# The last 65 keys of a cross-attention, split into 64 in half-array products and one by itself

## The chip, the cores and the metric

The kernel runs on one core of one Trainium2 chip. The metric is the device time of one execution in microseconds. The unchanged kernel took 3020.45, 3022.51 and 3024.7 us in three runs, a median of 3022.51.

A core has these engines, under the names that the profile uses: PE (TensorE, matrix products) with PEld (its weight loads), DVE (VectorE), ACT (ScalarE), POOL (GpSimd) and SP (SyncE, which issues most DMAs). A name with a q behind it (SPq, ACTq) is that engine's queue as an issuer of DMAs. They run side by side and wait for each other through semaphores.

## The reference

The program is a two-layer Perceiver block. Only its first piece changes, a cross-attention of 8 batches, each with 64 queries of width 512 over 1601 keys, in 16 heads of width 64:

```python
q = x @ Wq.T                              # (8, 64, 1024)
k, v = split(context @ Wkv.T, 2)          # (8, 1601, 1024) each
sim = einsum('bhid,bhjd->bhij', q, k) * 64**-0.5
sim = where(mask, sim, -max)
out = einsum('bhij,bhjd->bhid', softmax(sim), v)
return out @ Wout.T + b_out
```

All of it is in fp32. What follows it (a second attention with a Fourier transform and convolutions, experts, another cross-attention, another attention and a quantized feed-forward) is not touched.

## The kernel before

The keys are never projected. The query side is multiplied with the key weights once (`qk`, 512 x 512 for eight heads of a batch), so that the scores are `context @ qk`; and `softmax @ context` is made first (`a`) and multiplied with the value weights afterwards (`v_ps`).

The work goes in 16 **steps**, a step being one batch and one half of the heads, so that the 512 columns of a step are 8 heads by 64 queries. The loop over `step` at the end of `l0_xattn` lays out, for each step: load `qk` (`queries_of`, from a DRAM copy) and the columns of the context (`load_columns`), then `scores` of this step, then `attend` of the step before, then `softmax` of this step. So the matrix engine works at `attend` of the last step while the vector and scalar engines work at the softmax of this one. The Tile framework's scheduler turns this program order into one fixed list per engine, and interleaves the two steps at their seams. I call the seam at which `scores` of one step ends and `attend` of the step before begins a **passage**, and number it by the step whose `qk` is loaded there, 1 to 15.

1536 of the 1601 keys are multiplied by Strassen-Winograd's method in blocks of 256 x 512: seven products instead of eight, on quarters (`Quarters`, `Run`). GpSimd makes the sums of the context's quarters (`Quarters.left`, lines 136 to 139), and those of the queries' quarters (`right_of`, lines 222 to 225). Results of the products are taken out of PSUM by ScalarE (copies, line 439) and VectorE (sums, line 444), and VectorE keeps a running maximum `m` (line 460).

The other 65 keys, the **tail**, are multiplied plainly: in `scores` by four products of 128 columns of weights by 512 columns (line 472; 63 of the 128 weight columns are zeros), and in `attend` by eight products with 65 rows by 256 columns (line 605), four for each of two blocks, placed among the others by the class `Mixed`, which adds them to the same PSUM banks where it can.

PSUM is split into four pools of two banks each: `ps_x`, `ps_y`, `ps_z` for the seven products, and `ps_m` for all else: tail, `m_ps` (transposes of the maximum, line 498), `top_ps` (its broadcast, line 503), sums and values. The tile `qk` has one buffer: its next load is issued when the last product that reads it is done. Each fp32 product appears in the trace as two matmul records; an "x4" of a row is two products.

Of the kernel before, what the change touches and what calls it, by code (L numbers as in the profile page):

```python
# [120 lines left out]
NPAIR = LAST // 2  # L121

# [19 lines left out]
def l0_xattn(K, x, d, ternary, kept):  # L142
# [7 lines left out]
    with ExitStack() as es:  # L150
# [10 lines left out]
        ctxT_tail = wp.tile([P, DC, P], F32, tag="ctxT_tail", name="ctxT_tail")  # L161
        nc.gpsimd.memset(ctxT_tail, 0.0)
        ctx_tail = wp.tile([P, D], F32, tag="ctx_tail", name="ctx_tail")
        bias = wp.tile([P, B, NK], F32, tag="bias", name="bias")
        qk_all = [dp.tile([P, n, DC, NG, 2, S], F32, tag=f"qk_all{n}", name="qk_all") for n in (2, B - 2)]
        sp = es.enter_context(tc.tile_pool(name="a_s", bufs=2))
        tp = es.enter_context(tc.tile_pool(name="a_t", bufs=2))
        zp = es.enter_context(tc.tile_pool(name="a_z", bufs=1))

# [41 lines left out]
        def load_tails(b):  # L211
            nc.sync.dma_start(
                ctxT_tail[:, :, :TAIL], d["ctxT"][b, :, LAST * P :].rearrange("(c p) n -> p c n", p=P)
            )
            nc.sync.dma_start(ctx_tail[:TAIL], d["ctx"][b, LAST * P :, :])
# [78 lines left out]
        wqT = sp.tile([P, NK, HALF], F32, tag="s", name="wqT")[:, :8, :].rearrange("p (c j) n -> p c (j n)", j=2)  # L294
        wk = sp.tile([P, NK, HALF], F32, tag="s", name="wk")[:, :NG, :]
# [15 lines left out]
        m32 = wp.tile([B * NK, P], F32, tag="m32", name="m32")  # L311
        nc.scalar.dma_start(m8, d["mask"])
        load_tails(0)
        ctxT = load_columns(0)
        place = [tp.tile([P, 4, 3, QH], F32, tag="pt", name="stage").rearrange("p a b q -> p (a b q)") for _ in range(2)]
# [25 lines left out]
        for j in range(2):  # L341
# [17 lines left out]
        nc.vector.tensor_copy(m32, m8)  # L359
        ps = ps_m.tile([P, B * NK], F32, tag="mm", name="m_ps")  # L360
        nc.tensor.transpose(ps, m32, K.ident[: B * NK, : B * NK])
        nc.vector.tensor_scalar(
            bias.rearrange("p b k -> p (b k)"), ps, 1.0, -MASKED, ALU.subtract, ALU.mult
        )

# [65 lines left out]
        class Scores:  # L431
# [25 lines left out]
            def c21(self, ps):  # L457
                nc.scalar.activation(self.s[:, self.k + 1, :QH], ps, AF.Identity, bias=self.bias[1], scale=1.0)  # L458
                for k in (self.k, self.k + 1):
                    nc.vector.tensor_max(self.m, self.m if k else self.s[:, LAST, :], self.s[:, k, :])  # L460

        def scores(b, qkt, ctxT):
            qk, qt = qkt
            s = sp.tile([P, NK, HALF], F32, tag="s", name="s")
# [5 lines left out]
            ps = ps_m.tile([P, HALF], F32, tag="mm", name="s_ps")  # L470
            for c in range(DC):
                nc.tensor.matmul(ps, lhsT=ctxT_tail[:, c, :], rhs=qk[:, c, :], start=c == 0, stop=c == DC - 1)  # L472
            nc.scalar.activation(s[:, LAST, :], ps, AF.Identity, bias=bias[:, b, LAST : LAST + 1], scale=1.0)
            run = Run()
            for i in range(NPAIR):

                def mul(ps, n, start, i=i):
                    for e in range(2):
                        nc.tensor.matmul(  # L479
                            ps,  # L480
                            lhsT=ctxT[i][:, Quarters.LEFT[n], ts(e, P)],
                            rhs=right[n][:, e, :],
                            start=start and e == 0,
                            stop=e == 1,
                            skip_group_check=not start,
                        )

                run.add(mul, Scores(s, m, b, i))
                some(2)
                next(aside, None)  # L490
            run.end()
            return s, m
# [13 lines left out]
        def softmax(s, top):  # L506

            parts = []
            for k in (LAST, *range(0, LAST, 2)):
                n = min(2, NK - k)  # L510
# [15 lines left out]
            nc.vector.tensor_add(total[:TAIL], total[:TAIL], s[:TAIL, LAST, :])  # L526
            return parts, total

        class Mixed:
# [3 lines left out]
            def __init__(self, a, m, first, tail):  # L533
                self.a, self.m, self.first, self.tail = a, m, first, tail
# [4 lines left out]
            def keep(self, out, ps, h, n):  # L539
                if self.first:  # L540
                    nc.scalar.copy(out, ps)
                else:
                    nc.vector.tensor_add(out, ps, self.of(h, n))
# [7 lines left out]
            def p5(self, out, ps):  # L551
                if self.first:
                    w = ps_m.tile([P, HALF], F32, tag="mm", name="w_ps")[:, :QH]
                    self.tail(w, 1, 1, True)
                    nc.scalar.copy(out, w)
                    nc.vector.tensor_add(out, ps, out)
                else:
                    self.keep(out, ps, 1, 1)

            def c11(self, ps, p1):  # L560
                if self.first:
                    self.tail(ps, 0, 0, False)
                nc.vector.tensor_add(self.of(0, 0), ps, p1)

            def c12(self, ps, u2):
                if self.first:
                    self.tail(ps, 0, 1, False)
# [5 lines left out]
            def c21(self, ps):  # L573
                if self.first:
                    self.tail(ps, 1, 0, False)
                    nc.scalar.copy(self.of(1, 0), ps)
                else:
                    nc.vector.tensor_add(self.of(1, 0), ps, self.of(1, 0))

        def attend(half, s, soft, ctx, o, first):  # L580

            a = tp.tile([P, DC, HALF], F32, tag="a", name="a", bufs=1)
            wvT = wp.tile([P, DC, HALF], F32, tag="wvT", name="wvT")
# [3 lines left out]
            parts, total = soft  # L587
            run = Run()
            for part, right in enumerate(parts):
                pairs = range(3 * part, 3 * part + 3)  # L590
                for m in range(2):
# [12 lines left out]
                    def tail(ps, h, n, start, m=m):  # L604
                        nc.tensor.matmul(
                            ps,
                            lhsT=ctx_tail[:TAIL, ts(2 * h + m, P)],
                            rhs=s[:TAIL, LAST, ts(n, QH)],
                            start=start,
                            stop=True,  # L610
                            skip_group_check=not start,
                        )

                    run.add(mul, Mixed(a, m, part == 0, tail))
# [9 lines left out]
            nc.vector.reciprocal(rs, sums)  # L624
# [11 lines left out]
            nc.vector.tensor_mul(o[:, ts(half, NG // 2)], ps, rs)  # L636
# [22 lines left out]
        for step in range(2 * B + 1):  # L659
            if step < 2 * B:  # L660
                b, half = divmod(step, 2)
                if step:
                    now, ctxT = queries_of(b, half), load_columns(b, half)
                    if half == 0:
                        nc.sync.dma_start(
                            ctxT_tail[:, :, :TAIL], d["ctxT"][b, :, LAST * P :].rearrange("(c p) n -> p c n", p=P)
                        )
                s, m = scores(b, now, ctxT)
# [3 lines left out]
            if before:  # L672
                b0, half0 = divmod(step - 1, 2)
                attend(half0, *before, load_rows(b0), o[:, :, b0 % 2, :], step == 1)
                if half0 and b0 + 1 < B:
                    nc.sync.dma_start(ctx_tail[:TAIL], d["ctx"][b0 + 1, LAST * P :, :])
            if step < 2 * B:
                before = s, softmax(s, top)
# [1666 lines left out]
def layout(i):  # L2345
# [10 lines left out]
        "mask": np.pad(i["mask_BxS2_bf1"].view(np.uint8), ((0, 0), (0, NK * P - NKV))).reshape(B * NK, P),  # L2356
        "L0x_WqT": i["L0_xattn_Wq"].T,
# [72 lines left out]
```

## Time and profile before

| what | value |
|---|---|
| median of three runs | 3022.51 us |
| the profiled execution, its device time | 3019.59 us |
| its span, first to last instruction | 3017.8 us |
| PE busy | 2953.5 us (98% of the span), 15393 records |
| DVE, ACT, POOL busy | 61%, 28%, 28% of the span |
| granted TensorE clock, mean | 0.991 |

The cross-attention fills the first 1478 us of the span. The page's 40 slices show how even that stretch is:

```profile
PE   8999999999999999999999999999999999999897
PEld 6767778888888888888654446778788888888664
DVE  4845555666666666666533343487677676676838
ACT  2322232222232322222201222233333323323224
POOL 3341341424335342424110002322412404224011
```

A digit is the busy share of a slice of 75 us in tenths. The first twenty slices are the cross-attention: the matrix engine has no slice under 9 after the first, the vector engine stands mostly at 5 to 6, and the other two lower.

### The profile page before, as it was taken

The page shows a single profiled execution, that of the slowest core. Times are in us where ns is not written, and L with a number is a line of the kernel's source. Part 1 is how long each engine was busy: PE and PEld are TensorE (multiplying, and loading weights), DVE is VectorE, ACT ScalarE, POOL GpSimd, SP SyncE. Part 2 cuts the span into 40 slices and gives each one's busy share as a digit, 9 for nine tenths or more (in the row PEclk, how much of TensorE's full clock was granted, in tenths as well). Part 3 has the DMA queues.
Part 4 walks back from the last instruction along what each step waited for, and adds up shares of the span by engine and source line. Part 5 has one row for each costly group of instructions (what it writes and reads, how often), then busy time and mean ns, then how long its engine had stood idle before and what let it go on. Part 6 is the DMA issues. An engine that isn't in the chain of part 4 may idle for free.

```text
span 3017.8 us, 40186 instructions
## 1 busy us (share of the span) xinstructions
PE 2953.5 (98%) x15393; PEld 2263.7 (75%) x15393; DVE 1828.9 (61%) x3122; ACT 844.9 (28%) x1620; POOL 850.1 (28%) x766
## 2 busy tenths in 40 slices
PE   8999999999999999999999999999999999999897
PEld 6767778888888888888654446778788888888664
DVE  4845555666666666666533343487677676676838
ACT  2322232222232322222201222233333323323224
POOL 3341341424335342424110002322412404224011
PEclk9999999999999999999999999999999999999989
DMA  9275465544545564442649974202112021020260
GB/s 331 83 231 168 126 218 186 191 161 167 190 157 188 189 206 161 170 140 93 230 167 351 342 257 147 82 27 76 37 58 78 5 90 53 29 90 11 108 83 15
DMA packets 287725, 429.43 MB, mean 142 GB/s; under 512 B 50830, under 2 KB 187030, under 8 KB 283310
## 3 DMA queue, kind: packets, MB, share of 16 engines
q1 hardware_dynamic: 272345, 388.56, 38.6%
q10 hardware_dynamic: 14549, 36.21, 3.5%
q8 instruction: 122, 2.00, 0.3%
q0 software_dynamic: 640, 2.10, 0.2%
q14 instruction: 69, 0.57, 0.1%
HBM read 351.77 MB, written 75.04 MB: 141 GB/s over the span
## 4 chain that ended last, share of the span: by engine, by line
PE 92%; DVE 4%; DMA 1%; ACT 1%; issue 1%; POOL 0%; SPq 0%; POOLq 0%; DVEq 0%; ACTq 0%
PE x_ps L595 11%; PE x_ps L1529 11%; PE x_ps L479 11%; PE y_ps L1529 8%; PE s_ps L1699 6%; PE z_ps L479 5%; PE z_ps L595 5%; PE oe_ps L1244 4%; PE h_ps L1217 4%; PE acc L1754 3%; PE y_ps L595 3%; PE y_ps L479 3%; PE s_ps L472 2%; PE qk_ps L257 1%; PE v_ps L629 1%; PE sum_ps L1576 1%
## 5 line engine op out<-in xcount | busy, mean ns | idle before, releaser
L1589 POOL TENSOR_TENSOR r<-r,minus_half 128x52 f32<-128x52 f32 x32 | 277.0, 8673 | 552.6 <-DVE r L1588 552.6
L479 PE MATMUL x_ps<-qt,ctxT 128*128 128x256 f32 x1152 | 284.6, 381 | 2.3 <-DVE s L444 2.3
L595 PE MATMUL x_ps<-pt,ctx 128*128 128x256 f32 x1152 | 280.3, 381 | 0.0
L136 POOL TENSOR_TENSOR ctx<-ctx 128x256 f32<-128x256 f32 x96 | 74.2, 772 | 626.4 <-DMA ctx<-in_ctx 375.9
L479 PEld LDWEIGHTS x_ps<-qt,ctxT 128*128 128x128 f32 x1152 | 217.3, 190 | 40.2 <-issue 4.7
L595 PEld LDWEIGHTS x_ps<-pt,ctx 128*128 128x128 f32 x1152 | 216.5, 189 | 33.7 <-DVE a L568 1.6
L1699 PE MATMUL s_ps<-qb,kT 128*128 128x256 f32 x832 | 201.3, 382 | 0.1
L460 DVE TENSOR_TENSOR m<-m,s 128x512 f32<-128x512 f32 x176 | 138.4, 786 | 95.2 <-ACT s L458 92.8
L1699 PEld LDWEIGHTS s_ps<-qb,kT 128*128 128x128 f32 x832 | 155.0, 190 | 27.5 <-issue 4.9
L444 DVE SCALAR_TENSOR_TENSOR s<-y_ps,bias,p 128x256 f32<-128x256 f32 x96 | 46.4, 483 | 153.4 <-PE y_ps L479 153.0
L1709 DVE TENSOR_TENSOR s<-s_ps,r 128x512 f32<-128x512 f32 x192 | 126.7, 683 | 13.9 <-PE s_ps L1699 11.6
L511 DVE TENSOR_TENSOR s<-s,top_ps 128x1024 f32<-128x1024 f32 (+1 forms) x112 | 123.2, 1136 | 12.0 <-PE top_ps L503 12.0
L1739 DVE TENSOR_TENSOR s<-s,top_ps 128x1792 f32<-128x1792 f32 x64 | 117.9, 1884 | 16.5 <-PE top_ps L1735 16.3
L1740 ACT ACTIVATE s<-s 128x1792 f32<-128x1792 f32 x64 | 101.1, 1591 | 66.2 <-DVE s L1739 66.2
L1754 PE MATMUL acc<-s,v 128*64 128x128 f32 x1664 | 115.6, 280 | 3.7 <-ACT s L1740 3.7
L512 ACT ACTIVATE s<-s 128x1024 f32<-128x1024 f32 (+1 forms) x112 | 110.3, 996 | 29.7 <-DVE s L511 25.7
L1754 PEld LDWEIGHTS acc<-s,v 128*64 128x64 f32 x1664 | 98.1, 139 | 27.0 <-issue 22.6
L1217 PE MATMUL h_ps<-w,tok 128*128 128x512 f32 x256 | 117.3, 593 | 0.0
L1244 PE MATMUL oe_ps<-w,hT 128*128 128x512 f32 x256 | 115.6, 593 | 0.0
L525 DVE TENSOR_TENSOR total<-total,s 128x512 f32<-128x512 f32 x160 | 111.3, 695 | 3.7
L1236 ACT ACTIVATE hT<-hT_ps,L0f_be,L0f_g 128x128 f32<-128x128 f32 x128 | 55.4, 456 | 179.8 <-PE hT_ps L1235 116.9
L479 PE MATMUL x_ps<-qk,ctxT 128*128 128x256 f32 x384 | 103.5, 387 | 0.0
(470 smaller groups left out, 6116.1 us busy)
## 6 DMA issues: line engine op xcount, KB each, us to landing
w<-in_L0f_W SPq DMA_DIRECT2D x64, 1024.0 KB, 6.8
ctx<-in_ctx SPq DMA_DIRECT2D x192, 256.0 KB, 3.4
kept<-ctxT SPq DMA_DIRECT2D x48, 896.0 KB, 10.1
ctxT<-kept SPq DMA_DIRECT2D x48, 896.0 KB, 7.8
ctxT<-kept SPq DMA_DIRECT2D x24, 1792.0 KB, 7.8
ctxT<-in_ctxT SPq DMA_DIRECT2D x96, 256.0 KB, 4.9
wvT<-in_L0x_WvT SPq DMA_DIRECT2D x16, 1024.0 KB, 8.8
qk<-qk_all SPq DMA_DIRECT2D x15, 1024.0 KB, 6.6
```

The lines of the kernel that those rows point to most:

```text
L460: nc.vector.tensor_max(self.m, self.m if k else self.s[:, LAST, :], self.s[:, k, :])
L479: nc.tensor.matmul(ps, lhsT=ctxT[i][:, Quarters.LEFT[n], ts(e, P)], rhs=right[n][:, e, :], start=start and e == 0, stop=e == 1, skip_group ...
L511: nc.vector.tensor_sub(s[:, k : k + n], s[:, k : k + n], top.unsqueeze(1).to_broadcast([P, n, HALF]))
L595: nc.tensor.matmul(ps, lhsT=ctx[pair][:, Quarters.LEFT[n], ts(m, P)], rhs=right[n][:, i, :], start=start and i == 0, stop=i == 2, skip_gro ...
L1217: nc.tensor.matmul(ps, lhsT=self.tok[:, c, :], rhs=self.w1[n][:, c, :], start=c == 0, stop=c == DC - 1)
L1244: nc.tensor.matmul(ps, lhsT=self.hT[:, f, :], rhs=self.w2[f // 4][:, f % 4, :], start=f == 0, stop=f == 15)
L1529: nc.tensor.matmul(ps, lhsT=left(n, e), rhs=right(n, e), start=start and e == 0, stop=e == 1, skip_group_check=not start,)
L1589: nc.gpsimd.tensor_tensor(r, r, minus_half, ALU.pow)
L1699: nc.tensor.matmul(ps[:, i].rearrange("p h q -> p (h q)"), lhsT=kT[c][:, ts(k0 + i, P)], rhs=qb[c].rearrange("p h q -> p (h q)"), start=Tr ...
L1709: nc.vector.tensor_mul(out, ps, by)
L1739: nc.vector.tensor_sub(part, part, top.to_broadcast([P, n, 2 * P]))
L1754: nc.tensor.matmul(acc[ds(64 * j, 64), c, :], lhsT=v[:, k, ds(c * P + 64 * j, 64)], rhs=s[:, k, ts(j, P)], start=k == 0, stop=k == NK - 1,)
```

## The change

The 65 tail keys become 64 and one.

The **64** are multiplied in halves of the array. In `scores`, 64 weight columns take half of the array's columns, so the heads are split in two groups (`of_heads`), and one group's product goes to partitions 0 to 63 of the result and the other's to 64 to 127. In the new `attend_tail`, 64 rows take half of the array's rows, and the two groups go to two PSUM banks. The result is copied by ScalarE into `a`, ahead of `attend`, and `Mixed` always adds to `a` instead of starting it.

The **one** key's scores are a weighted sum of the rows of `qk`: ScalarE scales four blocks (`by`, `by_c`), GpSimd adds them up, and a product with `ones` sums over partitions (`score_of_one`). Its value row (`v_left`) is made once for all batches and is added at the end of `attend`, with its weight added to the softmax's denominator.

The diff, cut to what the steps below speak of:

```diff
         def scores(b, qkt, ctxT):
             qk, qt = qkt
-            s = sp.tile([P, NK, HALF], F32, tag="s", name="s")
+            wide = sp.tile([P, WIDE], F32, tag="s", name="s")
+            s, tail, one = parts_of(wide)
+            by = tp.tile([P, HALF], F32, tag="by", name="by")
+            nc.scalar.activation(
+                by, qk[:, 0, :], AF.Identity, bias=bias_left[:, b : b + 1], scale=left[:, 0, b : b + 1]
+            )
+            for c in range(1, DC):
+                more = tp.tile([P, HALF], F32, tag="by", name="by_c")
+                nc.scalar.activation(more, qk[:, c, :], AF.Copy, scale=left[:, c, b : b + 1])
+                nc.gpsimd.tensor_add(by, by, more)
...
-            ps = ps_m.tile([P, HALF], F32, tag="mm", name="s_ps")
+            ps = ps_m.tile([P, HALF], F32, tag="mm", name="s_ps")[:, :QH]
             for c in range(DC):
-                nc.tensor.matmul(ps, lhsT=ctxT_tail[:, c, :], rhs=qk[:, c, :], start=c == 0, stop=c == DC - 1)
-            nc.scalar.activation(s[:, LAST, :], ps, AF.Identity, bias=bias[:, b, LAST : LAST + 1], scale=1.0)
+                for h in range(2):
+                    nc.tensor.matmul(
+                        ps[ds(h * H2, H2)], lhsT=ctxT_tail[:, c, :], rhs=of_heads(qk[:, c, :], h),
+                        start=c == 0, stop=c == DC - 1,
+                    )
+            nc.scalar.activation(tail, ps, AF.Identity, bias=bias_tail[:, b : b + 1], scale=1.0)
+
+            def score_of_one():
+                ps = ps_m.tile([P, HALF], F32, tag="mm", name="one_ps")[:, :QH]
+                for h in range(2):
+                    nc.tensor.matmul(ps[ds(h * H2, H2)], lhsT=ones, rhs=of_heads(by, h), start=True, stop=True)
+                nc.scalar.copy(one, ps)
...
             def keep(self, out, ps, h, n):
-                if self.first:
-                    nc.scalar.copy(out, ps)
-                else:
-                    nc.vector.tensor_add(out, ps, self.of(h, n))
+                nc.vector.tensor_add(out, ps, self.of(h, n))
...
+        def attend_tail(wide):
             a = tp.tile([P, DC, HALF], F32, tag="a", name="a", bufs=1)
+            _, tail, _ = parts_of(wide)
+            for c in range(0, DC, 2):
+                heads = [
+                    ps_m.tile([P, HALF], F32, tag="mm", name="a_ps").rearrange("p (i n) -> p i n", i=2) for _ in range(2)
+                ]
+                for i in range(2):
+                    for h in range(2):
+                        r = ds(h * H2, H2)
+                        nc.tensor.matmul(
+                            heads[h][:, i], lhsT=ctx_tail[r, ts(c + i, P)], rhs=tail[r], start=True, stop=True
+                        )
+                for h in range(2):
+                    nc.scalar.copy(
+                        a[:, c : c + 2].rearrange("p i (g h q) -> p i g h q", h=2, q=S)[:, :, :, h, :],
+                        heads[h].rearrange("p i (g q) -> p i g q", q=S),
+                    )
+            return a
...
-            nc.vector.reciprocal(rs, sums)
+            one = one.rearrange("p (g q) -> p g q", q=S)
+            nc.vector.tensor_add(rs, sums, one)
+            nc.vector.reciprocal(rs, rs)
+            if b == 0:
+                ps = ps_m.tile([P, NG // 2, B], F32, tag="mm", name="left_ps")
+                for g in range(NG // 2):
+                    for c in range(DC):
+                        nc.tensor.matmul(
+                            ps[:, g, :], lhsT=wvT[:, c, ts(g, P)], rhs=left[:, c, :], start=c == 0, stop=c == DC - 1
+                        )
+                nc.vector.tensor_copy(v_left[:, ts(half, NG // 2)], ps)
...
-            nc.vector.tensor_mul(o[:, ts(half, NG // 2)], ps, rs)
+            o = o[:, ts(half, NG // 2)]
+            for g in range(NG // 2):
+                at = half * (NG // 2) + g
+                nc.vector.scalar_tensor_tensor(
+                    o[:, g], one[:, g], v_left[:, at, b : b + 1], ps[:, g], ALU.mult, ALU.add
+                )
+            nc.vector.tensor_mul(o, o, rs)
...
-                s, m = scores(b, now, ctxT)
+                wide, m = scores(b, now, ctxT)
+            if before:
+                b0, half0 = divmod(step - 1, 2)
+                a = attend_tail(before[0])
+                if half0 and b0 + 1 < B:
+                    load_rows_tail(b0 + 1)
+            if step < 2 * B:
                 top = top_of(m)
```

Besides, the maximum, the subtraction of the maximum and the sum over keys treat the two new parts in two halves of 64 partitions, which makes each of these one or three VectorE instructions longer than the single one on 512 columns, and the tail's loads fetch 64 keys, the context rows twice.

In the built order of the changed kernel, the passages 5 to 8 and 10 to 15 but 12 have this shape on PE (counts are products) and on ScalarE; here passage 6:

```
PE     z_ps<-qk x2 | x_ps<-qt x2 | a_ps x3 | x_ps<-qt x2 | a_ps x5 | m_ps x4 | x_ps<-s x2 | top_ps x4
ScalarE  copy a (1st bank) | s<-x_ps | copy a (2nd) | copy a (3rd) | by<-qk | copy a (4th) | ... | by_c<-qk
```

In passages 3 and 4 the scalar list reads `by`, `by_c`, (`by_c`,) two copies, `by_c`, two copies; and GpSimd's list at passage 3 reads add, sub, sub, sub, add, sub, add, where the subs are those of `right_of` and the adds those of `by`.

## Prediction

> **What bounds the kernel.** I read the chain of waits first, then busy time by stretches, then the groups of instructions by shape, then the timeline of single passages (times in us; a timeline row has start, length, engine, line, and what it was).
>
> ```profile
> PE 92%; DVE 4%; DMA 1%; ACT 1%; issue 1%; POOL 0%; SPq 0%; POOLq 0%; DVEq 0%; ACTq 0%
> 440.00:785.00 345.00, 343.24 (x1764) 287.90 (x1764) 212.50 (x338) 95.38 (x190) 133.50 (x163) 1.00 0.51 176
> ```
>
> The first line is the chain by engine. The second is one stretch of the cross-attention: length, then busy time of PE, PEld, DVE, ACT and POOL. PE is idle for 1.8 us in 345, VectorE is 62% busy. So time on PE is time of the kernel here, and a new wait of PE is paid whole.
>
> **What is removed.** By shape:
>
> ```profile
> L472 PE MATMUL s_ps<-qk,ctxT_tail 128*128 128x512 f32 x128 | 62.4, 619 | 1.4 <-DMA qk<-qk_all 1.4
> L605 PE MATMUL w_ps<-s,ctx_tail 65*128 65x256 f32 x64 | 19.2, 380 | 0.0
> L52 ACT COPY stage<-qk_ps 128x512 f32<-128x512 f32 x4 | 2.3, 586 | 4.6 <-PE qk_ps L257 4.6
> L512 ACT ACTIVATE s<-s 128x512 f32<-128x512 f32 x16 | 10.1, 632 | 8.8 <-DVE s L511 8.8
> ```
>
> The 380 ns overlap; what counts is start to start. Four records of 256 columns take 0.86 us (timeline below: 521.88 to 522.75), 0.216 each; one of 512 takes 0.43. Removed: 128 x 0.43 = 55.0 us, and four L605 groups of 64, 256 x 0.216 = 55.3: **110 us**.
>
> **What the halves cost.** The kernel already has half-array products, by columns (sum_ps, v_ps) and by rows (qk_ps):
>
> ```profile
> 267.83 1.03 PE L595 MATMUL z_ps<-s,ctx 128*128 128x256 f32 x4
> 268.79 0.92 PE L257 MATMUL qk_ps<-qT,w 64*128 64x384 f32 x4
> 269.64 0.70 PE L595 MATMUL x_ps<-pt,ctx 128*128 128x256 f32 x2
> ...
> 272.31 0.65 PE L622 MATMUL sum_ps<-total,ones 128*64 128x256 f32 x4
> 272.80 0.28 PE L629 MATMUL v_ps<-a,wvT 128*64 128x64 f32 x4
> 273.01 1.56 PE L595 MATMUL x_ps<-pt,ctx 128*128 128x256 f32 x6
> 274.50 0.45 PE L629 MATMUL v_ps<-a,wvT 128*64 128x64 f32 x8
> 274.88 0.70 PE L479 MATMUL x_ps<-qk,ctxT 128*128 128x256 f32 x2
> 275.42 1.02 PE L472 MATMUL s_ps<-qk,ctxT_tail 128*128 128x512 f32 x2
> ```
>
> sum_ps has the new tail's shape: its four records take 0.49, not 4 x 0.216 = 0.86. Two halves do run side by side. But crossing to halves and back costs. From 273.01 to 275.42 are 2.41 us; the work in it is 8 x 0.216 + 8 x 0.029 = 1.96 (0.029 is half of 64 columns' 0.054, with a little for issue); of the 0.45 above it 0.10 is still the return from sum_ps, so that there and back is 0.35. For rows: 267.83 to 268.79 is 0.10 more than its work, 268.79 to 269.64 is 0.21 more than two slots of 0.32, and the return adds 0.10: 0.40.
>
> Here a rule is weighed. The Trainium skill, TensorEngine Tiling (Array Packing), "Theoretical Speedup", gives up to 2x for a dimension of 64; its "Key Properties" say a change of tiling mode drains the engine, and "PSUM Bottleneck" that tiling doesn't speed up evacuation. By 2x alone the tail would fall by 55 us, less 7 for the one key: 48 gained. The rows decide:
>
> - tail of scores, 8 slots of 0.216 in 16 steps: 27.7; the one key, 2 slots: 6.9; tail of attend, 8 slots: 27.7
> - in the built order a_ps stands mostly as 3 and 5 products around another, so that one in each group has no partner: 2 more slots, 13 steps: 5.6
> - crossings: counted in both built orders, column halves 46 before and 59 after, row halves 38 and 73: 13 x 0.35 + 35 x 0.40 = 18.6
> - left_ps, 64 records with 128 weight columns and 8 columns: logit_ps (line 1116) has this shape, its starts 0.11 apart in the timeline: 7.0
>
> Sum 93.5. **PE gains 16.6 us**, not 48. The bound on an unpaired half is 0.216 a slot more; side by side for a whole order of two and two, the 5.6 vanish.
>
> **Other engines.** VectorE takes, a step, 6 additions in place of ScalarE's copies (0.42 each), three net pieces of maximum (4 x 0.42 less 0.79), one subtraction (0.69), five pieces at the end (4 of 64 columns at about 0.22, 2 of 0.42, less one of 0.42), in sum 5.6 us: 62% becomes 69%. Hidden under PE; bare it would be 90 us. ScalarE loses 8 copies of 0.37, gains 4 scalings (0.63, nearest row L512) and 4 copies of 512 columns (0.59, row L52). GpSimd gains 3 additions of 1.28 (rows L222 to L225), 61 us in all, hidden by its 60% of idle time. The last step's end, with nothing beside it, gets 1 us. Tail DMAs: the same count and one more, not waited for, 0.
>
> **New waits**, all at the passage. Before, passage 6:
>
> ```profile
> 522.94 0.37 SPq L230 DMA_DIRECT2D qk<-qk_all  x1
> ...
> 532.17 1.28 POOL L222 TENSOR_TENSOR qt<-qk 128x512 f32<-128x512 f32 x1 [4.11 <-DMA qk<-qk_all]
> ...
> 521.88 1.03 PE L479 MATMUL z_ps<-qk,ctxT 128*128 128x256 f32 x4
> 522.75 1.03 PE L479 MATMUL x_ps<-qt,ctxT 128*128 128x256 f32 x4
> ...
> 527.53 0.66 PE L498 MATMUL m_ps<-ident,m 128*128 128x128 f32 x4 [0.31 <-DVE m L460]
> ...
> 528.98 0.65 PE L503 MATMUL top_ps<-ident,top 128*128 128x128 f32 x4
> ```
>
> The load of qk is issued at 522.94; GpSimd, which waits for it, starts 9.2 later, after top_ps. Today nobody on PE's path needs it there. Read in this way, the 15 loads give 7.8, 5.8, 7.8, 7.7, 9.2, 9.2, 8.5, 9.5, 5.9, 5.6, 6.4, 7.4, 7.6, 5.9, 6.0.
>
> (a) a_ps needs four banks and ps_m has two. The third can't start before the first's copy, nor the fourth before the second's: matmul's tail 0.16, copy 0.59, semaphores 0.15, partly behind s<-x_ps (0.47), against 0.86 of other products. About 0.5 in 13 steps: **6.5**.
>
> (b) ScalarE takes its list in order. `by`, which waits for qk, stands ahead of the fourth copy; top_ps needs the bank that this copy frees. PE from 522.75: product 0.86, crossing and 4 slots 1.26, product 0.86, crossing and 6 slots and (a) 2.20, m_ps at 527.93, top_ps (1.45 after it, as before) at 529.38, 6.4 after the issue. By the load: landing + `by` 0.54 start to start + copy 0.59 + 0.1. With landing 0.1 before GpSimd's start, the wait is that start less 5.3: passages 5 to 8, 10, 11, 13 to 15 give 3.9, 3.9, 3.2, 4.2, 0.3, 1.1, 2.3, 0.6, 0.7: **20**. The page's rule that ScalarE is strict first-in first-out (TensorE: Matmul & The Clock Gate, its table's row on queue depth) speaks against this change; no row of before shows ScalarE blocking PE so. Without it (b) is 0; I take it, since each list here is fixed.
>
> (c) Passages 3 and 4: copies stand behind `by_c`, whose two buffers wait for GpSimd's additions, behind `right_of`. Landing 7.7, by and by_c 1.1, add 1.3, three subs 3.8, add 1.3, by_c and copy 1.1: m_ps 16.3 after the issue. PE's own list there is about 10 long. 6 and 5.5: **11.5**.
>
> (d) Step 1 has no attend to cover it. one_ps, before the third block's y_ps, waits for landing, four subs and three rounds of by_c and add: 73.5 + 5.1 + 5.0 = 83.6; PE's list reaches it at 80.6. It replaces part of today's 1.8 at y_ps. Net **2.5**.
>
> Given back: m_ps waits 0.3 to 0.7 for the maximum in each passage today; with more products ahead these go: **-6**.
>
> **Sum**: -16.6 + 1 + 6.5 + 20 + 11.5 + 2.5 - 6 = +19. Against the profiled 3019.6: 3038.5. That run lay 2.9 under the median; on the median 3041.5, **3042**.
>
> **Rivals.** *Faster*: the load lands by 5.3 everywhere and GpSimd keeps up; (b) and (c) vanish, -16.6 + 1 + 6.5 + 2.5 - 6 = -12.6: 3010. For it: six loads are at 6.4 or less. Against: none of the 15 is at 5.3 today, and the transfers that share the DMA engines at passages 5 to 8 stay. 12%. *No pairs in rows*: a_ps runs one by one, 16 slots instead of 10: +21 more, 3063; sum_ps and qk_ps speak against it. 6%. *Contention*: in the same passage GpSimd's L139 took 1.18 instead of 0.73 while VectorE's maximum took 1.05 instead of 0.69; 48 more additions of 1.28 may delay maxima and additions, 0.4 to 1 a step: +6 to +16, 3048 to 3058; inside my range, past it 4%. *It doesn't do what it says* (halves not split): 2%, then L641 would show 128 rows. *Gain and waits cancel*: 10%.
>
> **Numbers.** Main case, 66%: 3029 to 3060. Low end 3021 takes in most of cancelling, high end 3063 the rows unpaired. Within 0.2% (6 us, about what can be told from no change) 10%, faster 12%, slower 78%.
>
> **What would show it.** s_ps records in pairs at one start; z or x products after a_ps 0.1 late; ScalarE idle before `by` until DMA qk in passages 5 to 8, and PE idle 3 to 4 us before top_ps there; 5 to 6 before a_ps and m_ps in passages 3 and 4. It is wrong if PE has under 10 us of new idle, or if loads land early.

## The result, and the profile after

| | before | after |
|---|---|---|
| median, us | 3023.6 (4 runs, 3020.5 to 3024.8) | 3071.5 (4 runs, 3064.7 to 3080.2) |
| ratio, with 95% interval | | 1.0162 (1.0132 to 1.0192) |
| the profiled execution: device time, span | 3019.6, 3017.8 | 3067.5, 3065.8 |
| start of the last record of the cross-attention (o_ps) in it | 1478.1 | 1525.3 |

The change makes the kernel 1.6% slower. The whole of it is in the cross-attention, which ends 47.2 us later; what follows takes 1540.5 us now and took 1539.7.

First the chain of waits of the kernel after, by engine, and then the busy time of its cross-attention as one stretch, with the same stretch of the kernel before ahead of it (start:end, length, busy time of PE, PEld, DVE, ACT and POOL with their records, mean granted clock, DMA share, GB/s).

```profile
PE 85%; DVE 6%; DMA 4%; POOL 2%; ACT 2%; issue 1%; SPq 0%; POOLq 0%; DVEq 0%; ACTq 0%
```

```profile
0.00:1478.10 1478.10, 1454.10 (x7443) 1187.95 (x7443) 889.95 (x1429) 378.09 (x748) 522.82 (x651) 1.00 0.52 175
```

```profile
0.00:1525.30 1525.30, 1463.90 (x7700) 1184.47 (x7700) 979.16 (x1690) 411.63 (x764) 597.29 (x698) 0.99 0.51 170
```

PE's share of the chain has fallen from 92% to 85%; DMA, VectorE, GpSimd and ScalarE have taken its place. Length less PE busy is PE's idle time: 24.0 before, 61.4 after, **37.4 more**. But PE is also busy for 9.8 longer, where I had forecast 16.6 less. The last columns hint at why: the mean clock fell from 1.00 to 0.99.

Where the idle time is, from the groups of instructions of PE in the cross-attention, kernel after (busy time and mean ns of one, then idle time just before, and what ended it):

```profile
L558 PE MATMUL top_ps<-ident,top 128*128 128x128 f32 x64 | 12.8, 335 | 16.7 <-ACT a L645 15.8 <-DVE top L555 0.8
...
L526 PE MATMUL x_ps<-qt,ctxT 128*128 128x256 f32 x1152 | 287.1, 383 | 12.6 <-DVE s L465 12.6
...
L641 PE MATMUL a_ps<-s,ctx_tail 64*128 64x256 f32 x256 | 53.2, 411 | 8.2 <-ACT a L645 8.1
...
L553 PE MATMUL m_ps<-ident,m 128*128 128x128 f32 x64 | 11.2, 302 | 5.2 <-ACT a L645 3.7 <-DVE m L484 1.4
...
L516 PE MATMUL one_ps<-by,ones 128*64 128x256 f32 x64 | 11.4, 395 | 2.2 <-POOL by L498 2.2
```

The same groups in the kernel before (there is no a_ps and no one_ps in it):

```profile
L503 PE MATMUL top_ps<-ident,top 128*128 128x128 f32 x64 | 10.3, 284 | 0.8 <-DVE top L500 0.8
L479 PE MATMUL x_ps<-qt,ctxT 128*128 128x256 f32 x1152 | 284.6, 381 | 2.3 <-DVE s L444 2.3
L498 PE MATMUL m_ps<-ident,m 128*128 128x128 f32 x64 | 10.2, 282 | 6.6 <-DVE m L460 6.4
```

The rows of top_ps, a_ps and m_ps after the change are, for the most part, waits for a copy of `a` by ScalarE (15.8, 8.1 and 3.7). The row of x_ps waits for VectorE, 12.6 where it was 2.3. Passage 6 in the timeline shows both, and what the wait does (start, length, engine, line, what; in brackets the idle time before and what ended it). ScalarE first, then PE:

```profile
558.24 1.07 ACT L645 COPY a<-a_ps 128x512 f32<-128x512 f32 x2 [0.15 <-PE a_ps L641]
564.10 0.81 ACT L492 ACTIVATE by<-qk,bias_left,left 128x512 f32<-128x512 f32 x1 [4.78 <-DMA qk<-qk_all]
564.82 0.56 ACT L645 COPY a<-a_ps 128x512 f32<-128x512 f32 x1
```

```profile
556.45 1.13 PE L526 MATMUL x_ps<-qt,ctxT 128*128 128x256 f32 x4 [0.36 <-DVE s L465]
557.51 1.14 PE L641 MATMUL a_ps<-s,ctx_tail 64*128 64x256 f32 x6
558.88 1.13 PE L641 MATMUL a_ps<-s,ctx_tail 64*128 64x256 f32 x4 [0.24 <-ACT a L645]
559.94 0.66 PE L553 MATMUL m_ps<-ident,m 128*128 128x128 f32 x4
560.43 1.03 PE L665 MATMUL x_ps<-s,ctx 128*128 128x256 f32 x4
565.44 1.12 PE L558 MATMUL top_ps<-ident,top 128*128 128x128 f32 x4 [3.98 <-ACT a L645]
566.35 1.06 PE L665 MATMUL x_ps<-s,ctx 128*128 128x256 f32 x2
567.20 2.14 PE L665 MATMUL z_ps<-pt,ctx 128*128 128x256 f32 x6
```

Three copies of `a` are done, then ScalarE stands for 4.78 us at `by`, which waits for the load of qk; the fourth copy stands behind it, and top_ps behind the copy. That is the forecast wait. What I had not forecast is the last row: six records of 256 columns take 2.14, where six take 1.46 elsewhere. Three stretches of 3.41 us in the same place say why; the figure to read is the third from the end, the granted clock.

```profile
561.74:565.15 3.41, 0.00 (x0) 0.00 (x0) 0.00 (x0) 1.05 (x2) 1.00 (x1) 1.00 0.57 200
565.15:568.56 3.41, 3.12 (x10) 2.68 (x11) 1.69 (x3) 2.93 (x6) 3.33 (x4) 0.50 0.00 0
568.56:571.97 3.41, 3.41 (x17) 3.01 (x16) 2.96 (x5) 0.63 (x1) 3.33 (x5) 1.00 0.02 5
```

After a stretch in which PE did nothing, TensorE runs at half its clock for one stretch, and PE gets through 10 records instead of 17. In the cross-attention such half-clock time is 6.8 us before and 41.0 after. PE is busy in 6.8 and 35.6 of it, and half of that is lost.

So the 47.2 us come apart in three, each from these records: idle +37.4; half clock (35.6 - 6.8) / 2 = +14.4; and PE's work, counted at full clock (busy less half of the busy half-clock time), 1446.7 instead of 1451.3 = -4.6.

### The profile page after: what moved, and what is told of

It reads as the page before. It is cut to its first block, busy times and chain, and to the rows that moved or that the text cites. A ratio compares the mean times of both kernels' runs of the same rounds, so it can differ in the third digit from the quotient of the medians.

```text
span 3065.8 us, 41049 instructions
## 1 busy us (share of the span) xinstructions
PE 2965.6 (97%) x15650; PEld 2261.9 (74%) x15650; DVE 1917.8 (63%) x3383; ACT 878.3 (29%) x1636; POOL 924.6 (30%) x813
## 4 chain that ended last, share of the span: by engine, by line
PE 85%; DVE 6%; DMA 4%; POOL 2%; ACT 2%; issue 1%; SPq 0%; POOLq 0%; DVEq 0%; ACTq 0%
PE x_ps L1606 11%; PE x_ps L526 10%; PE x_ps L665 10%; PE y_ps L1606 8%; PE s_ps L1776 6%; PE z_ps L526 5%; PE z_ps L665 5%; PE oe_ps L1321 4%; PE h_ps L1294 4%; PE acc L1831 3%; PE y_ps L526 3%; PE y_ps L665 2%; DMA qk<-qk_all 2%; PE v_ps L699 1%; PE sum_ps L1653 1%
## 5 line engine op out<-in xcount | busy, mean ns | idle before, releaser
L526 PE MATMUL x_ps<-qt,ctxT 128*128 128x256 f32 x1152 | 287.1, 383 | 12.6 <-DVE s L465 12.6
L484 DVE TENSOR_TENSOR m<-m,s 128x512 f32<-128x512 f32 x160 | 131.0, 819 | 78.3 <-ACT s L479 76.2
L1776 PEld LDWEIGHTS s_ps<-qb,kT 128*128 128x128 f32 x832 | 155.0, 190 | 27.2 <-issue 4.9
L575 DVE TENSOR_TENSOR s<-s,top_ps 128x1024 f32<-128x1024 f32 x96 | 115.9, 1210 | 0.4
L1606 PE MATMUL y_ps<-ctxT,L1x_WkT 128*128 128x256 f32 x384 | 102.2, 381 | 0.0
```

Source lines behind the costliest of these rows:

```text
L484: nc.vector.tensor_max(self.m, self.m, self.s[:, k, :])
L526: nc.tensor.matmul(ps, lhsT=ctxT[i][:, Quarters.LEFT[n], ts(e, P)], rhs=right[n][:, e, :], start=start and e == 0, stop=e == 1, skip_group ...
L575: nc.vector.tensor_sub(s[:, k : k + n], s[:, k : k + n], top.unsqueeze(1).to_broadcast([P, n, HALF]))
L1606: nc.tensor.matmul(ps, lhsT=left(n, e), rhs=right(n, e), start=start and e == 0, stop=e == 1, skip_group_check=not start,)
L1776: nc.tensor.matmul(ps[:, i].rearrange("p h q -> p (h q)"), lhsT=kT[c][:, ts(k0 + i, P)], rhs=qb[c].rearrange("p h q -> p (h q)"), start=Tr ...
```

## The experiments

Theory **W**: the waits behind the scalings of the one key (`by`, `by_c`), and the half clock that follows them, make most of the loss. Theory **H**: the half-array products themselves make it. Theory **V**: VectorE's added maxima make it. Each experiment edits the kernel after. Times of the experiments are medians of 5 to 21 runs; the ratio is to the kernel before, run beside it on the same chip (medians 3019.1 to 3021.7), and its excess over 1 is what compares. Idle, half clock and work are those of the cross-attention up to the end of its last o_ps record, in the profiled execution:

| kernel | time | ratio (95%) | end | idle | half clock | work |
|---|---|---|---|---|---|---|
| before | 3023.6 | 1 | 1478.7 | 24.0 | 6.8 | 1451.3 |
| after | 3071.5 | 1.0162 (1.0132 to 1.0192) | 1525.8 | 61.4 | 41.0 | 1446.7 |
| e1 one key left out | 3023.9 | 1.0008 (0.9998 to 1.0019) | 1484.3 | 36.4 | 30.7 | 1432.9 |
| e2 scalings after the evacuation | 3082.9 | 1.0202 (1.0182 to 1.0221) | 1538.5 | 64.0 | 58.0 | 1450.4 |
| e3 other banks | 3039.5 | 1.0070 (1.0049 to 1.0092) | 1490.9 | 42.8 | 20.5 | 1439.0 |
| e4 tail's maxima early | 3073.9 | 1.0180 (1.0162 to 1.0198) | 1526.7 | 56.8 | 51.2 | 1446.5 |
| e5 scalings behind the copies | 3041.0 | 1.0069 (1.0054 to 1.0083) | 1498.5 | 38.7 | 23.9 | 1448.6 |
| e6 e3, e5, all maxima early | 3029.7 | 1.0034 (1.0022 to 1.0045) | 1485.9 | 39.1 | 17.1 | 1439.4 |
| e7 filler in the stalls | 3071.0 | 1.0163 (1.0146 to 1.0181) | 1527.7 | 52.6 | 44.4 | 1455.8 |
| e8 left loaded early | 3080.2 | 1.0197 (1.0184 to 1.0210) | 1545.9 | 74.9 | 68.3 | 1444.5 |
| e9 e6, left early, maxima spread | 3032.8 | 1.0041 (1.0025 to 1.0056) | 1490.4 | 43.1 | 30.7 | 1438.0 |
| e10 e9, steps 0 and 1 late | 3017.7 | 0.9986 (0.9978 to 0.9995) | 1478.8 | 33.2 | 20.5 | 1437.3 |

**e1, no one key.**

```diff
-            by = tp.tile([P, HALF], F32, tag="by", name="by")
...
-                nc.gpsimd.tensor_add(by, by, more)
...
-                for h in range(2):
-                    nc.tensor.matmul(ps[ds(h * H2, H2)], lhsT=ones, rhs=of_heads(by, h), start=True, stop=True)
-                nc.scalar.copy(one, ps)
+                nc.vector.memset(one, 0.0)
```

> The changed kernel without the one key's score: its four ScalarE scalings, GpSimd's additions and the two products of one_ps are left out, and its score is 0 for every query (the output is not the reference's). Theory W (waits behind the scalings, and the half TensorE clock that follows a stall of 3 to 4 us, make most of the loss): TensorE's idle time ahead of top_ps falls from 16.7 us to under 3, the half-clock windows of the cross-attention from 41 us to under 25, the time to about 3022 (3014 to 3032), of which some 12 us are the 15 x 0.78 us of one_ps itself. Theory H (the half-array products and their changes of shape make the loss, stalls are incidental): only the 12 us of one_ps go, about 3059. Theory V (VectorE's four added maxima ahead of the sum in the passage): about 3059 as well, x_ps still waits for VectorE.

The time is 3023.9, at theory W's figure; H and V are out as the main cause. The waits ahead of top_ps for ScalarE are gone and PE's work fell by 13.8. But half clock fell only to 30.7: with the stalls at ScalarE gone, x_ps waits 16.1 us for VectorE where it waited 12.6, in single gaps of up to 2.3 us. So the one key costs nearly all of the loss, 13.8 of it as work of PE, yet VectorE is the next late one.

**e2, the scalings after the tail's evacuation.**

```diff
             nc.scalar.activation(tail, ps, AF.Identity, bias=bias_tail[:, b : b + 1], scale=1.0)
+            by = tp.tile([P, HALF], F32, tag="by", name="by")
+            nc.scalar.copy(by[0:1, 0:1], tail[0:1, 0:1])
...
-                if first and i == NPAIR - 2:
+                if i == NPAIR - 2:
                     score_of_one()
```

> All the work of the changed kernel; only the place of the one key's scalings moves: each step issues them behind its own evacuation of the 64 keys, and the products of one_ps stand ahead of the last product of the scores, as step 0 has them. Theory W: the waits of 16.7 us ahead of top_ps, some 5 us in passages 3 and 4 and 2.4 us at one_ps go, and 10 to 15 us that the half clock added: about 3038 (3028 to 3046). Theory H and theory V: the same products, changes of shape and maxima are there, so 3066 to 3074.

Slower than the kernel after, against every theory. The waits ahead of top_ps did go; 27.2 us ahead of x_ps, ended by ScalarE's `p`, came. In step 6, ScalarE:

```profile
592.82 0.34 ACT L460 COPY p<-z_ps 128x256 f32<-128x256 f32 x1
593.71 0.37 ACT L460 COPY u<-x_ps 128x256 f32<-128x256 f32 x1 [0.55 <-PE x_ps L525]
600.46 0.72 ACT L511 ACTIVATE by_c<-qk,left 128x512 f32<-128x512 f32 x1 [6.37 <-POOL by L512]
...
602.55 0.72 ACT L511 ACTIVATE by_c<-qk,left 128x512 f32<-128x512 f32 x1 [1.37 <-POOL by L512]
...
603.18 0.35 ACT L460 COPY p<-x_ps 128x256 f32<-128x256 f32 x1
```

`by` and `by_c` share two buffers, so the next scaling needs GpSimd to have added the one before, and GpSimd was on twelve sums of the context's quarters from 589.09 to 599.17. An evacuation stands behind the scaling, and x_ps starts 4.82 late. A scaling blocks ScalarE for one of two causes, the load of qk and GpSimd's list; I had moved it clear of the first and into the second.

**e3, other banks for the third and fourth a_ps.**

```diff
-                    ps_m.tile([P, HALF], F32, tag="mm", name="a_ps").rearrange("p (i n) -> p i n", i=2) for _ in range(2)
+                    pool.tile([P, HALF], F32, tag=tag, name="a_ps").rearrange("p (i n) -> p i n", i=2)
+                    for pool, tag in (((ps_m, "mm"), (ps_m, "mm")) if c == 0 else ((ps_z, "z"), (ps_y, "y")))
```

> The changed kernel with the third and fourth a_ps banks taken from the pools ps_z and ps_y instead of ps_m, so that the last two copies of a gate neither m_ps nor top_ps; the scalings stay ahead of those copies. Theory W: the idle of 16.7 us (top_ps) and 5.2 us (m_ps) and the half clock after them go, unless the first products of attend wait for the banks instead: about 3040 (3030 to 3050). Theory H and theory V: 3066 to 3074.

3039.5, at W's figure, but this edit did more than I had meant. In passages 5 to 15 the built order now has all four copies of `a` ahead of `by`, so that the copies are moved as well as the banks. Passage 6, ScalarE, this kernel:

```profile
541.67 1.56 ACT L646 COPY a<-a_ps 128x512 f32<-128x512 f32 x3 [0.15 <-PE a_ps L642]
...
547.46 0.81 ACT L492 ACTIVATE by<-qk,bias_left,left 128x512 f32<-128x512 f32 x1 [1.19 <-DMA qk<-qk_all]
```

Only in passages 3 and 4 do copies still stand behind a `by_c`, and m_ps waits 1.73 and 2.18 us for them there. So e3 doesn't tell what the banks alone are worth to top_ps; e5, which moves the copies and leaves the banks, is the clean test of W. What e3 does show is a second gain, which I had not expected here. PE's work falls by 7.7 with the same products. The group of a_ps and passage 6, PE, this kernel:

```profile
L642 PE MATMUL a_ps<-s,ctx_tail 64*128 64x256 f32 x256 | 43.9, 406 | 0.1
```

```profile
540.94 1.56 PE L642 MATMUL a_ps<-s,ctx_tail 64*128 64x256 f32 x10
```

256 records keep PE busy for 43.9 instead of 53.2. Ten records run in 1.56, with 1.64 to the start of m_ps; in the kernel after the same ten are cut in two by a wait of only 0.24 for a bank and take 2.43, from 557.51 to 559.94. There the six ahead of the wait take four slots of 0.216 and the four behind it four more, where the ten take six here: the wait parts an upper half from the lower half that would have run beside it.

**e4, the 64 keys' maxima early.**

```diff
-                if i == NPAIR - 1:
+                if i in (2, NPAIR - 1):
-                        for rest in (tail, one):
+                        for rest in (tail if i == 2 else one,):
```

> The changed kernel with the 64 keys' two maxima taken at the third product of the scores, so that VectorE has two rather than four maxima of 64x256 ahead of the last sum of the scores. Theory V: the waits of x_ps for VectorE go, some 10 us: 3058 to 3064. Theory W: the 16.7 us ahead of top_ps and the half clock stay; the time falls by 2 to 8 us, 3063 to 3069. Theory H: 3068 to 3074.

x_ps waits 8.3 instead of 12.6 for VectorE, and the time does not fall, so V is out as the main cause: PE reaches top_ps earlier and waits there longer, 18.4 instead of 16.7. By itself this edit is worth nothing while a later wait in the passage ends the stall.

**e5, the scalings behind the copies of a.**

```diff
             by = tp.tile([P, HALF], F32, tag="by", name="by")
+            if marks:
+                nc.scalar.copy(by[0:1, 0:1], marks[-1][0:1])
...
+            mark = tp.tile([P, 1], F32, tag="mark", name="mark")
+            nc.scalar.copy(mark[0:1], a[0:1, DC - 2, S : S + 1])
+            marks.append(mark)
```

The last three lines stand at the end of `attend_tail`; the element read is one that the fourth copy writes.

> All the work of the changed kernel; each step's scalings are only tied behind the fourth copy of a (a one-element copy of a, which `by` starts from), so that the copies no longer stand behind them in ScalarE's list. GpSimd's additions, the products, the banks and the maxima are as in the changed kernel. Theory W (what is lost is the copies' place behind the scalings, with the half clock that follows): idle ahead of top_ps, m_ps and a_ps together falls from 30 us to under 10, the half-clock windows from 41 us to under 20, the time to about 3038 (3030 to 3046). Theory G (it is GpSimd's late additions that are paid, wherever the scalings stand, as when they stood behind the 64 keys' evacuation): the wait moves to the next user of ScalarE, and the time stays at 3065 or above.

3041.0: W holds. Idle ahead of top_ps, m_ps and a_ps falls from 30.1 to 5.6; half clock falls to 23.9, where under 20 was forecast. Passage 6, ScalarE, this kernel:

```profile
543.89 0.58 ACT L649 COPY a<-a_ps 128x512 f32<-128x512 f32 x1 [0.73 <-PE a_ps L645]
...
548.55 0.80 ACT L494 ACTIVATE by<-qk,bias_left,left 128x512 f32<-128x512 f32 x1
549.26 0.61 ACT L574 ACTIVATE s<-s 128x512 f32<-128x512 f32 x1
557.27 0.72 ACT L499 ACTIVATE by_c<-qk,left 128x512 f32<-128x512 f32 x1 [7.40 <-POOL by L500]
```

ScalarE still stands 7.40 at a `by_c` for GpSimd, but only exponentials (L574) are behind it, not a copy or an evacuation. GpSimd's lateness is paid only by what is behind it in ScalarE's list. PE's work is still 1448.6, 9.6 more than in e3, which also has its copies ahead: two banks part the pairs as in the kernel after.

**e6, e3 and e5 with all four maxima at the fourth product.** The two edits above, and `if i == (NPAIR - 1 if first else 3)` for the maxima.

> Three edits at once on the changed kernel: scalings behind the copies of a, the third and fourth a_ps banks from ps_z and ps_y, and all four added maxima taken at the fourth product of the scores rather than at the end. If the losses are separate (copies behind scalings, two banks, VectorE's maxima), each edit brings its own: idle of the cross-attention falls to about 25 us, as before the change, half clock to about 7 us, PE's full-clock work to about 1438, the time to 3008 to 3020, level with the kernel before or up to 0.4% faster. If they only cover for each other (a wait removed shows the next one), it stays at 3028 or above.

Missed: 3029.7. PE's work is as expected (1439.4), idle is not: 39.1 rather than 25. The start of step 0 showed a third place. ScalarE, kernel e6:

```profile
44.69 0.81 ACT L494 ACTIVATE by<-qk,bias_left,left 128x512 f32<-128x512 f32 x1 [4.75 <-DMA left<-in_left]
...
48.11 0.35 ACT L460 COPY p<-z_ps 128x256 f32<-128x256 f32 x1
```

`by` waits 4.75 for the load of `left`, the last one issued at the start, with evacuations behind it; z_ps stands 3.47. In the kernel after these two are 4.10 and 2.41, and m_ps of step 0 comes at 75.5 instead of 70.0. Also, four maxima in one place make x_ps wait 1.4 to 1.7 us there in four steps.

**e7, filler in the stalls.**

```diff
             nc.vector.tensor_reduce(top, ps, AX.X, ALU.max)
+            if fill:
+                ps = ps_z.tile([P, HALF], F32, tag="z", name="fill_ps")
+                for i in range(12):
+                    nc.tensor.matmul(ps[:, :P], lhsT=K.ident, rhs=K.ident, start=True, stop=True)
```

`fill` is true in passages 5 to 8.

> The changed kernel with 12 added products of the identity with itself (128x128, about 2.6 us), read by nobody, between m_ps and top_ps in passages 5 to 8, where TensorE stands idle for 2.7 to 4.1 us. No wait is taken away: top_ps still waits for the same copy. If the half clock after such a stall is a cost of its own: the 20 us of half-clock windows right after these four stalls go, and the end of the cross-attention comes 7 to 10 us earlier, time 3062 (3057 to 3067). If the half clock costs nothing by itself: no gain, 3069 or above, and more if the added products delay top_ps.

No gain in the time, so the figure missed. Locally the clock did what was expected: of the 17.1 us of half clock after these four stalls 3.4 stayed, and from top_ps on in passage 5 the first twenty records of 256 columns need 7.57 in the kernel after and 4.81 here (5.67 for 24, less four at 0.216). The gain was spent at once: the scheduler put the four x_ps records that used to stand in the stall behind it (0.86 a passage), VectorE is late at passage 8 (1.54), and later passages fell to half clock instead (1001, 1172). This run shows the half clock coming and going with the idle time, not a gain in total.

**e8, left loaded early.**

```diff
         nc.scalar.dma_start(m8, d["mask"])
+        nc.scalar.dma_start(left, d["left"])
...
-        nc.sync.dma_start(left, d["left"])
```

> The changed kernel with one DMA moved: the load of the last key's columns (left) is issued right behind the mask's, early, rather than last of the start's loads. If step 0 loses its 5 us (its m_ps comes at 75.5 instead of 70.0) because the first scaling waits for that load with four evacuations behind it in ScalarE's list: z_ps no longer waits 2.4 us near 48 us, the half clock after it goes, m_ps of step 0 comes at 70 to 72 and the time falls by 4 to 6 us, to 3065 to 3068. If GpSimd's additions are what holds ScalarE there: the wait stays, m_ps at 74 to 76, time 3069 to 3073.

Both figures missed, and the second theory was nearer: 3080.2. With left there, `by` starts at 23.2, then the second `by_c` stands 14.26 us until GpSimd is through 24 sums of the context, and PE stands 14 us. It is e2's wait again.

**e9, e6 with e8's load, maxima one at a time** at products 2 to 5.

> Four edits on the changed kernel: scalings behind the copies of a, the third and fourth a_ps banks from ps_z and ps_y, the load of left early, and the four added maxima taken one at a time at the second to fifth product of the scores (those of the one key in step 0 at the end). Against the kernel with the first two and all maxima at one product (3029.7): step 0 gains 5 us, the 1.5 to 1.8 us waits of x_ps for VectorE at that product go, some 5 us. If all of the loss is now accounted for: 3012 to 3022, 0.2% faster than the kernel before or level with it. If GpSimd's 48 additions or VectorE's 5.6 us a step are a floor of their own: 3025 or above.

Missed: 3032.8. e8's 14 us are in it (m_ps of step 0 at 85.7). Without them the steps are the fastest so far: from m_ps of step 1 to the end 1350.7, where the kernel before takes 1357.8. With the maxima spread, x_ps waits only 3.7 for VectorE, where it waited 12.6. So GpSimd's additions and VectorE's work are no floor of the steps.

**e10, and the scalings of steps 0 and 1 late.** left is loaded last again. `late` is true in steps 0 and 1; `scaled` issues one scaling and its addition, and s[0:1, 4] is written by the third product.

```diff
+                    nc.scalar.copy(by[0:1, 0:1], marks[-1][0:1] if marks else s[0:1, 4, 0:1])
...
+            late = not marks
...
+                if late:
+                    for c in range(DC) if i == NPAIR - 2 else ():
+                        scaled(c)
+                if late and i == NPAIR - 1:
                     score_of_one()
```

> As the kernel with scalings behind the copies of a, third and fourth a_ps banks from ps_z and ps_y and spread maxima, but left is loaded last as in the changed kernel, and in steps 0 and 1 the scalings start only once the third product of the scores is done (when left has landed and GpSimd is through its subtractions), with one_ps ahead of the last product. If the two starting steps lose time only because ScalarE stands before left and before GpSimd's additions with evacuations behind it: m_ps of step 0 comes at 70 to 72 (70.4 before the change, 78.0 with scalings early), that of step 1 at 119 to 124 (before 121.2), idle of the cross-attention falls to 22 to 28 us, the time to 3010 to 3020: level with the kernel before or up to 0.3% faster. If scalings anywhere in a step cost TensorE a like amount: 3025 or above.

**3017.7, 0.9986 of the kernel before: 0.14% faster (0.05% to 0.22%), and 1.7% faster than the change as it was made**, with all of its work. The gain rests on the timed runs: the profiled execution, at 3021.0, lay 3.4 above their median, and its cross-attention ends where that of before does. Step 0's m_ps is back at 69.7. Step 1's is not (127.0, before 120.8), and idle is 33.2 where 22 to 28 was forecast: z_ps waits 4.54 for a sum that stands behind the softmax's additions on VectorE. From step 5 to step 15 the lag behind the kernel before falls from 7.9 to 0.9 us, 0.7 a step: that is the change's own gain once its waits are gone.

## Why the prediction was right and wrong

The sign and the main mechanism were right; the time was not. 3042 was forecast, and 3071.5 is above my high end of 3063. In the sum's own terms:

| term of the sum | forecast | measured |
|---|---|---|
| (b) top_ps waits for the copy behind `by` | 20 | 15.8 |
| (c) passages 3 and 4 | 11.5 | 1.93 + 2.21 + 2.89 + 1.52 = 8.6 |
| (d) one_ps in step 1, net | 2.5 | 2.2 - 1.8 (y_ps, gone) = 0.4 |
| (a) two banks, as idle time | 6.5 | 8.2 - 4.8 (in (c)) = 3.4 |
| m_ps's wait for the maximum given back | -6 | 1.4 left of 6.6: -5.2 |
| VectorE | 0 | 12.6 - 2.3 = 10.3 |
| step 0, wait for left | not named | 2.4 + 1.0 = 3.4 |
| the last step's end, from its m_ps on | 1 | -0.2 |
| PE's work | -16.6 | -4.6 |
| half clock | not named | +14.4 |

The measured idle terms sum to 36.7, of 37.4 found; the rest lies in small groups. Four terms together came out 40 too low in the forecast: half clock, PE's work, VectorE and step 0. The waits (a) to (d) and the last step came out 13 to 14 too high, and it is luck that this covered part of it. Two of my sums are 0.2 off (110.3 less 93.5 is 16.8, and VectorE's pieces make 5.4 a step), which changes nothing here.

**(b) and (c) held in mechanism and place**, and were a fifth to a quarter too long: 3.95, 3.98, 3.20 and 2.55 in passages 5 to 8, where I had 3.9, 3.9, 3.2 and 4.2, but only 2.2 in the later ones, where I had 5. (d)'s wait came too, but all of today's 1.8 went in exchange. e5, which moves only the copies' place, takes back 28 us of about 49 (by the ratios). The Trainium skill's rule that ScalarE takes its list in order (TensorE: Matmul & The Clock Gate, the row on queue depth in its first table), which I had set beside a trace without such a case, agrees with the rows of passage 6: the copy whose bank was ready starts at 564.82, after the late `by`.

**The first failed step is one that isn't there: the clock.** I priced every stall by its length alone. Of the stalls of 2 to 4 us in the kernel after, nearly all are followed by one to three stretches at half clock, each of which costs up to 1.7 us (half of 3.41): 14.4 in all, half of the 28 by which the profiled sum was short (47.2 against 19). It could have been read from the kernel before:

```profile
391.66:395.07 3.41, 1.28 (x6) 0.78 (x5) 0.59 (x2) 0.85 (x2) 3.33 (x6) 1.00 0.98 367
395.07:398.48 3.41, 3.38 (x7) 1.70 (x8) 0.92 (x2) 0.48 (x1) 0.49 (x1) 0.50 0.77 240
```

Two stretches of the kernel before: 2.13 us of idle, then the clock at 0.50.

**The second is "Hidden under PE"** for VectorE's 5.6 us a step. The sum was right: its busy time grew by 89, where I had 90. Its mean load went from 60% to 64% (979.16 of 1525.30), and that much does hide; but four of its added instructions, 1.7 us, stand at the very place where the passage's fourth product waits for a sum, and PE stood 10.3 us more. e9, which spreads them, has 3.7 left of the 12.6. e4 shows that this isn't an independent price: it took away 4.3 of the wait and gained nothing.

**The third is the size of (a)** and with it PE's work. I counted the two banks as 6.5 of waiting and kept all pairs but one in each group of three and five. The idle was 3.4; the greater part came as work, 9.3 in a_ps's busy time, as a wait of 0.24 parts a pair. With the banks free the work falls by 12.3 (e3) to 14.0 (e10), near the 16.6 of the sum; the price of the halves and of their crossings, taken together, was right within some 3 to 4 us. What makes up these I haven't tried.

The rival *faster* needed early loads; in passage 6 `by` starts 9.86 after the load's issue (554.24), as late as before. *No pairs in rows*, which I gave 6%, is partly what happened, for the groups of five, and for a cause that I had not named. *Contention* is small: VectorE's maximum over 512 columns takes 819 ns on average where it took 786, some 5 us over its 160; whether any of that reached PE is not shown.

## What to carry to other kernels

An instruction that waits long did harm here not by its own lateness, but by what was queued behind it on its engine: put it behind the last instruction that another engine needs soon, and check everything that it waits for (here the load of each step, a buffer that another engine frees, and a load made once at the start), since moving it clear of one can move it into the next. After such an edit read the built order again: e3's edit of the banks moved the copies too. Price a stall of the matrix engine with the half clock after it, and read from the trace how long a stall brings it on. Where half-array products run in pairs, make sure that no wait, however short, can fall between the two of a pair.

## What the runs showed of the hardware

**Half clock after some 2 us of idle time in one stretch.** The stretches of 3.41 us lie on a fixed grid: the half-clock ones start at whole multiples of it from each other (49.74, 77.05, 244.30 in the kernel after). Over the twelve kernels here I counted the stretches of the cross-attention that ran at full clock, from the first clock record on, by PE's idle time in them: of those with 2.0 us or more, all 53 were followed by one at half clock; of those with 1.6 to 2.0, 14 of 29; with 1.0 to 1.6, none of 53; under 1.0, 8 of 4990. The Trainium skill (TensorE: Matmul & The Clock Gate, section "What's actually happening") gives one idle window of about 3.4 us as the condition; its window length agrees with these stretches, but here some 60% of a window is enough, and stalls in one window add up: in the kernel after, 1.38 ahead of m_ps and 0.79 ahead of top_ps were enough in the stretch from 73.64. A stall that falls across two stretches can pass: the 2.20 ahead of one_ps at 87.76 left 1.72 in the first of them, and brought none. By the page's condition, taken as a window wholly idle, only one of the eight half-clock episodes of the kernel after would come about, that of passage 6.

**Products of 8 columns did not keep the clock up.** The eight exceptions under 1.0 us are of one kind: left_ps, which the change added, stands as runs of 12 and 20 records in each of two steps, and each of the eight is a stretch that holds all of a run of 20. Of the 48 full-clock stretches with fewer of these records none was followed by half clock. One of the eight, in e10, first the run of 20 and then the two stretches:

```profile
174.91 2.29 PE L708 MATMUL left_ps<-left,wvT 128*128 128x8 f32 x20
```

```profile
173.88:177.29 3.41, 3.41 (x30) 3.26 (x30) 1.10 (x3) 0.00 (x0) 0.00 (x0) 1.00 0.44 96
177.29:180.70 3.41, 3.41 (x32) 2.46 (x31) 3.27 (x4) 0.37 (x1) 1.72 (x2) 0.50 1.03 277
```

The profile calls PE busy through the whole of the first, and the half clock comes all the same. It makes 6.8 of e10's 20.5 us of half clock, and 3.4 of it in e1, e4, e5, e6, e8 and e9 each; the kernel after has none from this cause. Why such products count like idle time here is not shown.

**A short wait costs more than its length in paired halves:** 0.24 us between two products turned 1.64 us for ten records (e3) into 2.43.
